# One state in four of a selective scan gets its input from TensorE instead of GpSimd, and several buffers are shared

## The chip, the cores and the metric

The kernel runs on one core of a Trainium2 chip. The metric is the device time of one execution in microseconds (us); less is better. PE is TensorE (PEld its weight loads), DVE is VectorE, ACT is ScalarE, POOL is GpSimd, SP is SyncE, which here does nothing but issue transfers. Each engine works through its own queue in order. PE writes its results to PSUM, which has eight banks of 128 partitions x 512 fp32 values.

## The reference

The input is x of 16 batches x 512 positions x 256 channels. Two layers follow each other: a selective state space model run in both directions, and a mixture of experts with soft slots; each is added to its input and normalised. Cut to what matters here:

```python
xr = x @ in_proj_w.T                     # 512 channels xf, 512 channels res
xf = silu(causal_conv(xf)); xb = silu(causal_conv(xf, other weights))
for u, reverse in ((xf, False), (xb, True)):
    dt, B, C = ...                       # dt: softplus, per channel; B, C: 16 states per position
    dA  = dt[l, d] * A[d, n]             # decay
    dBu = dt[l, d] * u[l, d] * B[l, n]   # what is added at each position
    h   = scan over l of exp(dA) * h + dBu     (with a damping factor)
    y  += sum over n of h[l, d, n] * C[l, n] + u * D
x1 = layernorm(x + (y * silu(res)) @ out_proj_w.T)
# then: 16 experts x 64 slots, softmax dispatch, gated expert layers, softmax combine, layernorm
```

So for each batch, direction, channel and state there is one scan over the 512 positions.

## The kernel before

Channels lie on the 128 partitions, the 512 positions along the free axis. The 512 channels are four chunks `c` of 128. For each batch `b` the function `scan_part` is called four times: chunks 0 and 1 forward (`r` = 0) and backward (`r` = 1), then chunks 2 and 3 forward and backward. A part goes through the 16 states two at a time (`n` = 0, 2, ..., 14). One *step* is one chunk and two states, so there are 64 steps in a batch and 1024 in all. A step does this:

- SP loads the two states' rows of B and C, broadcast over the partitions, into `bs` (three buffers) and `cs` (two buffers); one load serves two steps (L349).
- POOL forms `db` = `du` * `bs` for both states in one product of 128x1024 (L353); `du` = dt * u was made once per chunk and direction (L301).
- For each of the two states ACT writes the decay exp(A * dt) into a PSUM bank `h` (L358) and the damping factor `th` into SBUF (L360), DVE scans in place in that bank, `h` = scan(`h`, `db`) (L362 forward, L364 backward), and DVE forms `hg` = (`th` + 1) * `h` in SBUF (L367). The banks for `h` are a ring of three; `hg` has four buffers.
- POOL multiplies both states' `hg` by `cs` (L368).
- PE adds the product up over the states by eight transposes into the accumulator bank `acc` (L317); `add_up(2)` puts that two steps behind. Once in a chunk and direction PE adds u * D with a diagonal matrix `diagD` (L330): full fp32 products of 128x128.

The eight PSUM banks are: three for `h`, two for `acc`, three (`bank`) for everything else.

All the other work is cut into pieces by generators: `prep` (projections, convolution `taps`, B and C through `project_unit`, and dt, `rr`, `du` through `prep_pair` for the next part), `front` (`finish` of the batch before: output projection, normalisation, `dispatch` into slots) and `back` (`experts` of two batches, `combine` of each). `beside_scan` takes pieces of these after each step. Expert and combine work runs from batch 3 on; before that there is only `prep` and `front`. What is left of it after the last scan is the tail. A scheduler of the language places the instructions on each engine's queue from this program order, buffers and its own estimate of times; `late` fixes the place of the marked ones.

Buffers that the change touches: the x tile of a batch is loaded once and kept (two buffers) from `prep_forward` to `finish`; expert weights `W` have three buffers of 4 KB a partition; the slot embeddings `se` and the expert outputs `ceo` in `combine` share one of 8 KB; `et` and `sl` in `dispatch` have one each, `yt` in `finish` two.

Of the kernel before, what the change touches and what calls it, by code (L numbers as in the profile page):

```python
# [28 lines left out]
KW = 4  # L29
NE = 16  # L30
SL = 64
NSL = NE * SL
# [23 lines left out]
def seq_layers(tc, ident, neghalf, a, out):  # L56
# [17 lines left out]


    nc = tc.nc
    nb = a["x"].shape[0]
    with ExitStack() as ctx:
# [3 lines left out]
        s_dram = drams.tile([nb, NM, P, NSL], F32, name="s_dram")  # L82
        e_dram = drams.tile([NE, nb * SL, DM], F32, name="e_dram")
        const = ctx.enter_context(tc.tile_pool(name="m_const", bufs=1))
        p1 = ctx.enter_context(tc.tile_pool(name="m_p1", bufs=1))
# [19 lines left out]
        def load_x(b):  # L105
            xt = p2.tile([P, NL, DM], F32, tag="x", name=f"x_{b}")
            nc.sync.dma_start(xt, a["x"][b].rearrange("(c p) d -> p c d", p=P))
            return xt

        xs = {0: load_x(0)}  # L110


        outT = const.tile([P, ND, DM], F32, name="outT")
        zeros = const.tile([P, L], BF16, name="zeros")
        nc.vector.memset(zeros, 0.0)

        unit = const.tile([XW, 1], F32, name="unit")
# [69 lines left out]
        def prep_forward(b, lo, hi, out):  # L187

            xt = xs[b]
            if lo == 0:  # L190
                out["xT"] = p1.tile([P, NM, L], F32, tag="xT", name=f"xT_{b}")
                for k in range(NM):
                    yield 1
                    pt = bank(f"ptx_{b}_{k}")
                    for lc in range(NL):
                        nc.tensor.transpose(
                            pt[:, lc * P : (lc + 1) * P], xt[:, lc, k * P : (k + 1) * P], ident
                        )
                    yield HOLD
                    late(nc.scalar.copy(out["xT"][:, k, :], pt))  # L200
                out["u"] = p1.tile([P, ND, L], F32, tag="xf", name=f"xf_{b}")
            xT, xf = out["xT"], out["u"]
            for c in range(lo, hi):
                yield 1
                pp = project(xT, c, f"pin_{b}_{c}")
                yield HOLD
                taps(xf[:, c, :], pp, side[0], c, xf[:, c, :])
            if hi == ND:
                yield 0
                late(nc.scalar.activation(xf, xf, AF.Silu))  # L210
                yield from project_unit(b, 0, out)
# [25 lines left out]
        def project_unit(b, r, out):  # L237

            w = side[r]
            q = f"{b}_{r}"  # L240
            yield 1
            px = bank(f"px_{q}")
            for c in range(ND):
                nc.tensor.matmul(  # L244
                    px[:XW, :], w["xT"][:, c, :], out["u"][:, c, :], start=(c == 0), stop=(c == ND - 1)
                )
            yield HOLD
            xd = p1.tile([XW, L], F32, tag=f"xd_{r}", name=f"xd_{q}")
            bc = dram.tile([2, NS, L], F32, tag="bc", name=f"bc_{q}")
            if r == 0:  # L250
                late(nc.scalar.activation(xd, px[:XW, :], AF.Identity, bias=unit))
            else:

                late(nc.scalar.activation(xd[: XB + NS, :], px[: XB + NS, :], AF.Identity, bias=unit[: XB + NS]))
                nc.scalar.copy(xd[XC:XW, :], px[XC:XW, ::-1])
            nc.sync.dma_start(bc[0], xd[XB : XB + NS, :])
            nc.sync.dma_start(bc[1], xd[XC:XW, :])
            out.update(xd=xd, bc=bc)

        def prep_pair(b, r, p, v, gate=None):  # L260
# [27 lines left out]
            for c, q, pz in pzs:  # L288
# [12 lines left out]
                nc.gpsimd.tensor_tensor(du, dt, v["u"][:, c, :], ALU.mult)  # L301
                v[c] = (dt, rr, du)

# [34 lines left out]
        def scan_part(b, r, p, v, accs, done, then):  # L338

            prep.drain()  # L340
            prep.gens += [[1, g] for g in then]
            w = side[r]
            for n in range(0, NS, 2):
                q = f"{b}_{r}_{p}_{n}"

                bs = p3.tile([P, 2, L], F32, tag="bs", name=f"bs_{q}")
                cs = p3.tile([P, 2, L], F32, tag="cs", name=f"cs_{q}", bufs=2)
                for t, rows in ((bs, v["bc"][0, n : n + 2, :]), (cs, v["bc"][1, n : n + 2, :])):
                    nc.sync.dma_start(t, rows.unsqueeze(0).to_broadcast([P, 2, L]))  # L349
                for c in (2 * p, 2 * p + 1):  # L350
                    dt, rr, du = v[c]
                    db = p3.tile([P, 2, L], F32, tag="db", name=f"db_{q}_{c}")
                    nc.gpsimd.tensor_tensor(db, du.unsqueeze(1).to_broadcast([P, 2, L]), bs, ALU.mult)  # L353
                    hg = p3.tile([P, 2, L], F32, tag="hg", name=f"hg_{q}_{c}", bufs=4)
                    for j in range(2):
                        s = slice(n + j, n + j + 1)
                        h = ps_h.tile([P, L], F32, tag="h", name=f"h_{q}_{c}_{j}")
                        nc.scalar.activation(h, dt, AF.Exp, scale=w["A"][:, c, s])  # L358
                        th = p3.tile([P, L], F32, tag="th", name=f"th_{q}_{c}_{j}")
                        nc.scalar.activation(th, rr, AF.Tanh, bias=LN_1E12 / 2, scale=w["Ah"][:, c, s])  # L360
                        if r == 0:
                            nc.vector.tensor_tensor_scan(h, h, db[:, j, :], 0.0, ALU.mult, ALU.add)  # L362
                        else:
                            nc.vector.tensor_tensor_scan(  # L364
                                h[:, ::-1], h[:, ::-1], db[:, j, ::-1], 0.0, ALU.mult, ALU.add
                            )
# [3 lines left out]
                        (r == n == 0, n == 0, r == 1 and n == NS - 2, c, hg, accs, w, v["u"], f"acc_{q}_{c}", done)  # L370
                    )
                    evict()
                    beside_scan()
# [74 lines left out]
        def moe_setup():  # L448
# [4 lines left out]
            for t in (sg, sb):  # L453
                nc.vector.tensor_scalar(t, t, scale, None, ALU.mult)
            se = p1.tile([P, NSC, DM], F32, tag="ceo", name="se")
            nc.sync.dma_start(se, a["slot_embeds"].rearrange("e (s) d -> (e s) d").rearrange("(c p) d -> p c d", p=P))
            yield 0
            mv, rs = row_stats(nc, p1, se, neghalf, "se")
            sh = shifts(mv, rs, "se")
            yield 0  # L460
            scaled(se, se, sh, rs)
            for k in range(NM):
                for h in range(NSC // 4):
                    yield 1
                    pt = bank(f"pse_{k}_{h}")
                    for j in range(4):
                        nc.tensor.transpose(
                            pt[:, j * P : (j + 1) * P], se[:, h * 4 + j, k * P : (k + 1) * P], ident
                        )
                    yield HOLD  # L470
# [3 lines left out]
            for key in ("bg", "bu"):  # L474
                rows = p1.tile([NE * NF, P], F32, tag="et", name=f"{key}_rows")
                nc.sync.dma_start(rows, a[key].rearrange("e (c p) -> (e c) p", p=P))
# [23 lines left out]
        def finish(b, y):  # L500

            xt = xs.pop(b)
            for h in range(NL // 2):
                yts = []
                for lc in (2 * h, 2 * h + 1):
# [6 lines left out]
                    yield HOLD  # L512
                    yt = p2.tile([P, L], F32, tag="yt", name=f"yt_{b}_{lc}")
                    late(nc.scalar.copy(yt, pt))
# [49 lines left out]
        def dispatch(b, xn, x2T):  # L564

            for sc in range(NSC):
# [9 lines left out]
                late(nc.vector.reduce_max(nm, pl, AX.X, negate=True))  # L576
                et = p1.tile([P, L], F32, tag="et", name=f"et_{i}")
                sm = p3.tile([P, 1], F32, tag="sm", name=f"sm_{i}")
# [15 lines left out]
                if sc % 2 == 1:  # L594
# [12 lines left out]
                    yield HOLD  # L607
                    sl = p1.tile([P, NM, 256], F32, tag="sl", name=f"sl_{i}")
                    for k in range(NM):
# [137 lines left out]
        def combine(b):  # L747


            eo = p1.tile([P, NSC, DM + 1], F32, tag="ceo", name=f"ceo_{b}")  # L750
            nc.gpsimd.memset(eo[:, :, DM : DM + 1], 1.0)  # L751
            own = e_dram[:, b * SL : (b + 1) * SL, :]
            for j in range(2):
                nc.sync.dma_start(
                    eo[j * SL : (j + 1) * SL, :, :DM],
                    own.rearrange("(c j) s o -> j s c o", j=2)[j],
                )
            x1 = p1.tile([P, NL, DM], F32, tag="cx1", name=f"cx1_{b}")
# [7 lines left out]
            x2 = load_x2(0)  # L766
            yield 0
            prev = []

# [8 lines left out]
            for lc in range(NL):  # L778
# [40 lines left out]
                for sc in range(NSC):  # L819
                    nc.tensor.matmul(  # L820
                        po[:, : DM + 1],
                        cts[sc // 4][:, sc % 4 * P : (sc % 4 + 1) * P],
                        eo[:, sc, :],
                        start=(sc == 0),
                        stop=(sc == NSC - 1),
                    )
# [15 lines left out]
        for b in range(nb):  # L842
# [21 lines left out]
            if b + 1 < nb:  # L864
                xs[b + 1] = load_x(b + 1)
                then.append(prep_forward(b + 1, 0, 2, nxt))
# [64 lines left out]
```

## Time and profile before

| What | Value |
|---|---|
| Time, median of 3 runs | 5519.68 us (5513.75 to 5530.24) |
| Profiled execution: time | 5517.41 us |
| Profiled execution: span | 5515.6 us |
| PE busy, share of the span | 4004.2 us, 73% |
| DVE busy | 4522.2 us, 82% |
| ACT busy | 4097.3 us, 74% |
| POOL busy | 4998.6 us, 91% |
| Granted PE clock, mean | 0.861 |
| Data moved by transfers | 897.76 MB, mean 163 GB/s |

Busy is the time in which an engine was executing at least one instruction. The profile's rows have the line of the kernel, the engine, the operation, output and inputs by name, shapes and count, then the busy time and the mean length of one in ns, then how long the engine had idled just before them and what ended that idling. "A <- B" in a list of waits means that A's instruction was waiting and B's ended it; behind it stand the sum in us, how many times, and the longest. Matmuls overlap in their pipeline, so their mean length is longer than busy time over count. The chain of waits follows the work that ended last back to the start. The 40 slices give busy tenths per slice of 138 us.

### The profile page before, as it was taken

How to read it: one execution, taken by the hardware profiler on the slowest of the kernel's cores; microseconds unless marked ns; L12 is line 12 of the kernel's file. 1: busy time of each engine (PE TensorE's matmuls, PEld its weight loads, DVE VectorE, ACT ScalarE, POOL GpSimd, SP SyncE). 2: the span in 40 equal slices, each digit the busy share in tenths (PEclk: the TensorE clock that was granted, in tenths of full speed). 3: DMA queues.
4: the chain of work that ended last, by engine and by line, in shares of the span. 5: the costliest groups of instructions: out<-in, count | busy, mean ns of one | idle time of the engine just before them, and what ended most of it. 6: DMA issues, size and time to landing. Idle time of an engine off the chain costs nothing.

```text
span 5515.6 us, 67752 instructions
## 1 busy us (share of the span) xinstructions
PE 4004.2 (73%) x21330; PEld 3097.9 (56%) x21330; DVE 4522.2 (82%) x6210; ACT 4097.3 (74%) x6662; POOL 4998.6 (91%) x2525
## 2 busy tenths in 40 slices
PE   4556656777777777777777777777777777877777
PEld 3434444666556655666555655566556556566565
DVE  7787878888888889889888888888898898888512
ACT  6667677778778887878878787788778788777522
POOL 6999999999999999999999999999999999989500
PEclk7667777888988989888998899989899889999998
DMA  4333333565445654465545654456544665467253
GB/s 132 112 108 126 121 117 124 167 199 188 157 138 195 203 193 140 144 207 193 172 139 173 203 191 151 147 190 203 186 144 146 203 195 172 137 212 240 83 161 96
DMA packets 493852, 897.76 MB, mean 163 GB/s; under 512 B 44307, under 2 KB 291731, under 8 KB 493493
## 3 DMA queue, kind: packets, MB, share of 16 engines
q1 hardware_dynamic: 454836, 851.48, 47.6%
q10 hardware_dynamic: 38656, 41.95, 2.2%
q8 instruction: 169, 2.77, 0.2%
q14 instruction: 191, 1.56, 0.1%
HBM read 832.47 MB, written 60.82 MB: 162 GB/s over the span
## 4 chain that ended last, share of the span: by engine, by line
DVE 34%; ACT 24%; PE 18%; issue 11%; POOL 10%; DMA 3%; SPq 0%; DVEq 0%; ACTq 0%; POOLq 0%
DVE h L364 9%; DVE h L362 9%; DVE hg L367 8%; ACT h L358 5%; ACT th L360 5%; POOL hg L368 4%; POOL db L353 4%; PE acc L317 3%; PE px L244 2%; DVE rr L299 2%; PE cl L785 2%; PE pg L709 2%; ACT L358 2%; PE cpo L820 1%; ACT ht L731 1%
## 5 line engine op out<-in xcount | busy, mean ns | idle before, releaser
L353 POOL TENSOR_TENSOR db<-du,bs 128x1024 f32<-128x1024 f32 x1024 | 2431.3, 2374 | 113.8 <-DVE h L362 48.6
L368 POOL TENSOR_TENSOR hg<-hg,cs 128x1024 f32<-128x1024 f32 x1024 | 2427.6, 2371 | 25.4 <-DVE hg L367 17.6
L367 DVE SCALAR_TENSOR_TENSOR hg<-th,h 128x512 f32<-128x512 f32 x2048 | 1352.3, 680 | 251.1 <-ACT th L360 139.9
L317 PE MATMUL acc<-ident,hg 128*128 128x128 f32 x8192 | 1214.9, 301 | 391.4 <-POOL hg L368 316.0
L317 PEld LDWEIGHTS acc<-ident,hg 128*128 128x128 f32 x8192 | 1069.2, 157 | 634.1 <-POOL hg L368 410.9
L364 DVE TENSOR_TENSOR_SCAN h<-h,db 128x512 f32<-128x512 f32 x1024 | 1227.2, 1221 | 191.0 <-ACT h L358 155.2
L362 DVE TENSOR_TENSOR_SCAN h<-h,db 128x512 f32<-128x512 f32 x1024 | 1222.8, 1221 | 180.6 <-ACT h L358 131.7
L358 ACT ACTIVATE h<-dt,A_f 128x512 f32<-128x512 f32 x1024 | 699.9, 683 | 319.2 <-DVE hg L367 316.5
L358 ACT ACTIVATE h<-dt,A_b 128x512 f32<-128x512 f32 x1024 | 700.0, 684 | 292.6 <-DVE hg L367 290.9
L360 ACT ACTIVATE th<-rr,Ah_b 128x512 f32<-128x512 f32 x1024 | 728.0, 711 | 0.3
L360 ACT ACTIVATE th<-rr,Ah_f 128x512 f32<-128x512 f32 x1024 | 726.9, 710 | 0.2
L694 PE MATMUL peo<-Wd,ht 128*128 128x256 f32 x1024 | 314.8, 461 | 190.4 <-DVE ht L678 129.4
L694 PEld LDWEIGHTS peo<-Wd,ht 128*128 128x128 f32 x1024 | 223.2, 227 | 263.1 <-DVE ht L678 143.3
L709 PE MATMUL pg<-st,Wg 128*128 128x128 f32 x2048 | 277.7, 297 | 85.5 <-ACT xb L219 40.6
L785 PE MATMUL cl<-seT,cx 128*128 128x512 f32 x512 | 279.4, 689 | 75.3 <-DVE rr L299 36.7
L709 PEld LDWEIGHTS pg<-st,Wg 128*128 128x128 f32 x2048 | 265.7, 211 | 97.2 <-ACT xb L219 42.1
L666 PE MATMUL pu<-st,Wu 128*128 128x128 f32 x2048 | 270.2, 288 | 33.3 <-ACT ht L731 11.8
L666 PEld LDWEIGHTS pu<-st,Wu 128*128 128x128 f32 x2048 | 257.5, 203 | 57.0 <-ACT ht L731 16.8
L571 PE MATMUL pl<-x2T,seT 128*128 128x512 f32 x512 | 261.1, 634 | 22.9 <-DVE xf L168 12.5
L600 PE MATMUL pq<-dis,xn 128*128 128x256 f32 x1024 | 253.8, 405 | 15.7 <-ACT dis L590 13.0
L820 PE MATMUL cpo<-ceo,ct 128*128 128x257 f32 x1024 | 249.3, 398 | 21.9 <-ACT ct L814 17.0
L751 POOL MEMSET ceo<- 128x8 f32 x16 | 2.0, 124 | 260.4 <-PE cpo L820 259.4
(146 smaller groups left out, 5356.6 us busy)
## 6 DMA issues: line engine op xcount, KB each, us to landing
bs<-bc SPq DMA_DIRECT2D x512, 512.0 KB, 4.6
cs<-bc SPq DMA_DIRECT2D x512, 512.0 KB, 3.7
Wg<-in_Wg_dram SPq DMA_DIRECT2D x128, 512.0 KB, 5.4
Wu<-in_Wu_dram SPq DMA_DIRECT2D x128, 512.0 KB, 5.7
Wd<-in_Wd_dram SPq DMA_DIRECT2D x128, 512.0 KB, 5.6
bd<-in_bd_dram SPq DMA_DIRECT2D x128, 128.0 KB, 4.7
s_dram<-sl ACTq DMA_DIRECT2D x64, 256.0 KB, 2.9
st<-s_dram SPq DMA_DIRECT2D x128, 128.0 KB, 4.3
```

The costliest lines, as they stand in the source:

```text
L317: ins = nc.tensor.matmul(accs[c][:, s], hc[:, j, s], ident, is_transpose=True, start=False, stop=(last and j == 1 and lc == NL - 1),)
L353: nc.gpsimd.tensor_tensor(db, du.unsqueeze(1).to_broadcast([P, 2, L]), bs, ALU.mult)
L358: nc.scalar.activation(h, dt, AF.Exp, scale=w["A"][:, c, s])
L360: nc.scalar.activation(th, rr, AF.Tanh, bias=LN_1E12 / 2, scale=w["Ah"][:, c, s])
L362: nc.vector.tensor_tensor_scan(h, h, db[:, j, :], 0.0, ALU.mult, ALU.add)
L364: nc.vector.tensor_tensor_scan(h[:, ::-1], h[:, ::-1], db[:, j, ::-1], 0.0, ALU.mult, ALU.add)
L367: nc.vector.scalar_tensor_tensor(hg[:, j, :], th, 1.0, h, ALU.add, ALU.mult)
L368: nc.gpsimd.tensor_tensor(hg, hg, cs, ALU.mult)
L666: nc.tensor.matmul(pu[:, fc * P : (fc + 1) * P], got["Wu", e][:, k, fc * P : (fc + 1) * P], st[:, k, :, j * SL : (j + 1) * SL], start=(k = ...
L694: nc.tensor.matmul(po[:, :DM], ht[:, fc, :], got["Wd", e][:, fc, :], start=(fc == 0), stop=(fc == NF - 1))
L709: nc.tensor.matmul(pg[:, fc * P : (fc + 1) * P], got["Wg", e][:, k, fc * P : (fc + 1) * P], st[:, k, :, j * SL : (j + 1) * SL], start=(k = ...
L785: nc.tensor.matmul(cl, x2[:, k, :], seT[:, k, h * 512 : (h + 1) * 512], start=(k == 0), stop=(k == NM - 1),)
```

## The change

For one state in four (n = 3, 7, 11, 15) PE makes dt*u*B instead of POOL. `du` is transposed once per chunk and direction into `duT` (positions on partitions), and multiplied by diagonal matrices of B, one of 128x128 for each quarter of the positions. The result lands in an `h` bank; ACT writes the decay to an SBUF tile `dec`, and DVE scans with the bank as the addend, in place. The diagonal matrices come from a DRAM array that is zero but for its diagonals: it is filled with zeros at the start, `project_unit` writes the four states' rows of B onto the diagonals by one transfer of 2048 words, and `scan_part` loads the matrix of one state into `dg` once in four steps. In every second pair of states POOL's `db` product and the load of `bs` cover one state only.

To make room, x has one buffer and is loaded twice per batch; the slot embeddings and `combine`'s expert outputs are cut into pieces that use the buffers of `W`; `yt`, `et`, `sl` and the bias rows share two buffers `fr`; `combine`'s column of ones is set by DVE.

```diff
+        diag_dram = drams.tile([2, NS // 4, NL, DIAG_SIZE], F32, name="diag_dram")   # DIAG = 3, DIAG_SIZE = P * (P + 1)
...
         def load_x(b):
-            xt = p2.tile([P, NL, DM], F32, tag="x", name=f"x_{b}")
+            xt = p1.tile([P, NL, DM], F32, tag="x", name=f"x_{b}")
...
+        blank = p2.tile([P, 4 * DM], F32, tag="W", name="blank", bufs=3)
+        nc.vector.memset(blank, 0.0)
+        for part in diag_dram.rearrange("r i l (p s) -> (r i) p l s", p=P):
+            nc.scalar.dma_start(part, blank[:, : NL * (P + 1)].rearrange("p (l s) -> p l s", l=NL))
...
         def prep_forward(b, lo, hi, out):
-            xt = xs[b]
             if lo == 0:
+                xt = load_x(b)
...
         def project_unit(b, r, out):
...
             nc.sync.dma_start(bc[1], xd[XC:XW, :])
+            nc.scalar.dma_start(
+                diag_dram[r].rearrange("i l (p s) -> i l p s", p=P)[:, :, :, 0],
+                xd[XB + DIAG : XB + NS : 4, :].rearrange("i (l p) -> i l p", p=P),
+            )
...
         def prep_pair(b, r, p, v, gate=None):
...
-                v[c] = (dt, rr, du)
+                v[c] = [dt, rr, du]
+            yield 0
+            yield 0
+            yield 2
+            pts = []
+            for c, q, pz in pzs:
+                pt = bank(f"pdu_{q}")
+                for lc in range(NL):
+                    nc.tensor.transpose(pt[:, lc * P : (lc + 1) * P], v[c][2][:, lc * P : (lc + 1) * P], ident)
+                pts.append(pt)
+            yield HOLD
+            for (c, q, pz), pt in zip(pzs, pts):
+                duT = p2.tile([P, L], F32, tag="duT", name=f"duT_{q}", bufs=4)
+                late(nc.scalar.copy(duT, pt))
+                v[c].append(duT)
...
         def scan_part(b, r, p, v, accs, done, then):
+            made = {}
+            def by_diagonal(n, c):
+                made[n, c] = h = ps_h.tile([P, L], F32, tag="h", name=f"h_{b}_{r}_{n}_{c}")
+                for lc in range(NL):
+                    s = slice(lc * P, (lc + 1) * P)
+                    ins = nc.tensor.matmul(h[:, s], v[c][3][:, s], dg[:, s], start=True, stop=True)
+                    if lc == 0:
+                        late(ins)
+            chunks = (2 * p, 2 * p + 1)
             for n in range(0, NS, 2):
+                diag = n % 4 + 1 == DIAG
+                k = 2 - diag
-                for t, rows in ((bs, v["bc"][0, n : n + 2, :]), (cs, v["bc"][1, n : n + 2, :])):
-                    nc.sync.dma_start(t, rows.unsqueeze(0).to_broadcast([P, 2, L]))
-                for c in (2 * p, 2 * p + 1):
-                    dt, rr, du = v[c]
+                nc.sync.dma_start(bs[:, :k, :], v["bc"][0, n : n + k, :].unsqueeze(0).to_broadcast([P, k, L]))
+                nc.sync.dma_start(cs, v["bc"][1, n : n + 2, :].unsqueeze(0).to_broadcast([P, 2, L]))
+                if not diag:
+                    dg = p2.tile([P, L], F32, tag="dg", name=f"dg_{q}")
+                    nc.sync.dma_start(
+                        dg.rearrange("p (l s) -> p l s", l=NL),
+                        diag_dram[r, n // 4, :, : P * P].rearrange("l (p s) -> p l s", p=P),
+                    )
+                for c in chunks:
+                    dt, rr, du = v[c][:3]
-                    nc.gpsimd.tensor_tensor(db, du.unsqueeze(1).to_broadcast([P, 2, L]), bs, ALU.mult)
+                    nc.gpsimd.tensor_tensor(
+                        db[:, :k, :], du.unsqueeze(1).to_broadcast([P, k, L]), bs[:, :k, :], ALU.mult
+                    )
                     for j in range(2):
-                        h = ps_h.tile([P, L], F32, tag="h", name=f"h_{q}_{c}_{j}")
-                        nc.scalar.activation(h, dt, AF.Exp, scale=w["A"][:, c, s])
+                        if j < k:
+                            dec = h = ps_h.tile([P, L], F32, tag="h", name=f"h_{q}_{c}_{j}")
+                            add = db[:, j, :]
+                        else:
+                            add = h = made.pop((n + j, c))
+                            dec = p2.tile([P, L], F32, tag="dec", name=f"dec_{q}_{c}")
+                        nc.scalar.activation(dec, dt, AF.Exp, scale=w["A"][:, c, s])
...
-                            nc.vector.tensor_tensor_scan(h, h, db[:, j, :], 0.0, ALU.mult, ALU.add)
+                            nc.vector.tensor_tensor_scan(h, dec, add, 0.0, ALU.mult, ALU.add)
...
+                    if c == chunks[0] and diag:
+                        by_diagonal(n + 1, chunks[1])
+                    elif c == chunks[1] and not diag:
+                        by_diagonal(n + 3, chunks[0])
                     evict()
...
         def finish(b, y):
-            xt = xs.pop(b)
+            xt = load_x(b)
...
-            eo = p1.tile([P, NSC, DM + 1], F32, tag="ceo", name=f"ceo_{b}")
-            nc.gpsimd.memset(eo[:, :, DM : DM + 1], 1.0)
+            for c0 in range(0, NSC, 3):
+                m = min(3, NSC - c0)
+                t = p2.tile([P, 4 * DM], F32, tag="W", name=f"ceo_{b}_{c0}", bufs=3)
...
+            for t in eos:
+                late(nc.vector.memset(t[:, :, DM : DM + 1], 1.0))
```

## The prediction

> **What bounds the kernel now.** I read the page's totals and slices first, then busy times by stage, then the waits of each stage, then the chain. Totals and slices:
>
> ```profile
> PE 4004.2 (73%) x21330; PEld 3097.9 (56%) x21330; DVE 4522.2 (82%) x6210; ACT 4097.3 (74%) x6662; POOL 4998.6 (91%) x2525
> ...
> POOL 6999999999999999999999999999999999989500
> PEclk7667777888988989888998899989899889999998
> ```
>
> By these POOL is the bound: it is full from the second slice until the scan ends near 5190 us. The next two views contradict it for most of the span. Busy times of a stage early in the run (400 to 1000 us) and one after the expert work has joined (1000 to 4280 us); in brackets the instructions:
>
> ```profile
> 400.00:1000.00 600.00, 371.74 (x1670) 272.63 (x1669) 496.60 (x600) 430.85 (x675) 587.10 (x291) 0.73 0.36 121
> 1000.00:4280.00 3280.00, 2481.39 (x13654) 1938.88 (x13653) 2878.28 (x3949) 2617.71 (x4258) 3191.18 (x1602) 0.89 0.54 174
> ```
>
> The columns are PE, PEld, DVE, ACT, POOL, granted clock, DMA. A step (one channel chunk, two states) has 8 transposes at L317; the view of that line counts 976 in the early window and 5232 in the late one, so 122 and 654 steps: 4.92 and 5.02 us a step. A late step holds 4.88 us of POOL, 4.40 of DVE, 4.00 of ACT, 3.79 of PE. What PE waits for, early, then late:
>
> ```profile
> PE acc L317 <- POOL hg L368: 140.2, 61, 5.9
> PE acc L317 <- POOL rr L298: 20.3, 8, 3.5
> PE pd L585 <- ACT et L581: 16.8, 6, 5.0
> ...
> PE pd L585 <- ACT et L581: 99.3, 35, 7.3
> PE ctp L809 <- ACT cm L802: 97.4, 35, 9.1
> PE peo L694 <- DVE ht L678: 93.7, 32, 5.2
> PE acc L317 <- POOL hg L368: 39.1, 32, 2.2
> ```
>
> Early, 160 of PE's 228 us of waiting are for POOL. Late, 70 of 799 are (39.1 and 30.4); the rest is PE, in order, standing before side work whose operand ACT or DVE has not finished. The chain agrees. Early, then late:
>
> ```profile
> by line: POOL db L353 13.1%; issue 12.1%; POOL hg L368 11.8%; DVE h L364 10.9%; DVE h L362 9.7%; DVE hg L367 7.4%; PE acc L317 4.4%; ACT th L360 3.8%; PE pq L600 3.8%; ACT h L358 3.6%; DVE rr L299 1.7%; PE pz L268 1.6%; ACT L358 1.3%; PE px
> ...
> by line: issue 11.2%; DVE h L364 9.3%; DVE hg L367 9.2%; DVE h L362 8.8%; ACT h L358 5.8%; ACT th L360 5.4%; POOL hg L368 3.1%; PE acc L317 3.0%; POOL db L353 2.6%; PE px L244 2.4%; DVE rr L299 2.2%; PE pg L709 2.0%; ACT L358 1.9%; PE cl L7
> ```
>
> POOL's two products hold 25% of the early chain and 6% of the late one. So POOL sets the pace for about three batches of 16 (192 steps); for the other 832 steps it is just busy enough, and the pace comes from the ring ACT `h`, DVE scan, DVE `hg`, ACT `h` over three PSUM banks, with PE's in-order queue beside it:
>
> ```profile
> ACT h L358 <- DVE hg L367: 355.7, 284, 3.6
> ```
>
> **The change, part by part.** Rows used:
>
> ```profile
> L353 POOL TENSOR_TENSOR db<-du,bs 128x1024 f32<-128x1024 f32 x1024 | 2431.3, 2374 | 113.8 <-DVE h L362 48.6 <-issue 45.7 <-DVE h L364 10.7
> L301 POOL TENSOR_TENSOR du<-dt,xb 128x512 f32<-128x512 f32 x64 | 80.3, 1278 | 0.0
> L330 PE MATMUL acc<-diagD_f,xf 128*128 128x128 f32 x512 | 76.7, 299 | 0.0
> L330 PE MATMUL acc<-diagD_b,xb 128*128 128x128 f32 x512 | 71.9, 286 | 0.0
> L585 PE MATMUL pd<-ident,et 128*128 128x128 f32 x512 | 96.5, 320 | 163.3 <-ACT et L581 149.0 <-DVE xf L168 14.3
> ```
>
> *POOL.* 512 of the 1024 `db` products shrink from 128x1024 to 128x512. The nearest half-size product is `du`: 2374 - 1278 = 1096 ns, times 512, is 561 us off POOL, 0.55 a step: 4.88 becomes 4.33.
>
> *PE.* 512 banks of four full fp32 products. L330 is the same shape and shows 1024 instructions where the code has 512 products, so two each: (76.7 + 71.9) / 128 = 1.16 us a bank, 594 us in all. `duT` adds 512 transposes, at 96.5 / 512 us 97 us. Together 691 us, 0.67 a step: 3.79 becomes 4.46. PE goes from the least to the most loaded engine of a late step. Of these 0.67 us nothing is on the path if they all fall into PE's waits (1.22 us a late step, 0.11 of it for POOL); all of it is if each wait keeps its length, because its operand starts from an earlier PE result that is now later too. Bounds 0 and 0.67 x 832 = 557 us. I take a third, 185: the waits are some 3 us long and come every two to three steps, so one of them can take up most of what was added since the last, and what remains delays the next side operand.
>
> The clock bears on this: 0.73 is granted where PE is busy 62%, 0.89 at 76%, and a transpose of L317 costs 0.183 us of PE in the first window (178.83 / 976), 0.139 in the second (724.62 / 5232). The Trainium skill ("TensorE: Matmul & The Clock Gate", Part 1) says that the array's clock is halved after idle windows and released by sustained work. By that rule a fuller PE comes to full clock, its late work shrinks by a ninth or 0.4 us a step, and the 185 would be near 70. By the rows the late stage is near full clock already, and I count nothing.
>
> *The banks.* A made bank is taken from the ring of three when PE fills it, one place ahead of an `h` that DVE reads sooner, and returned after it. I took both kernels' built instruction orders and summed, for each ACT `h`, DVE's work between the `hg` that frees its bank and the scan that needs it, at busy time over count (scan 1.20, `hg` 0.66 us). That cover falls short of a lone `h` (0.68 us) by 1 us in all before and 51 after; of an `h` behind one `th` (0.68 + 0.71) by 32 and 124; behind two such pairs (2.8) by 386 and 758. DVE's recorded waits for ACT `h`, 287 us, lie between the last two. So the added wait is between 50 and 372 us; I take the middle row, 92, as ACT mostly issues `h` and `th` in pairs. The made bank itself has 5.9 us of cover in the mean and is rarely late.
>
> *ACT.* 128 `duT` copies at 579 ns (L590, same shape), 74 us; 512 `dec` written to SBUF, at the 26 ns between `th` and `h` 13 us; 32 issues of the diagonal's write. A 512-element issue of 4 bytes takes 0.5 us on SP (`cb_f`), one of 256 pieces 0.37, so some 1.5 us for 2048: 48 us. Together 135 us; behind each issue stand Softplus and the next `h`. A third on the path, as for PE: 45; bounds 0 and 135.
>
> *Transfers.* `dg` takes the bytes that `bs` loses. It is queued on SP among loads that wait for POOL, about four steps (20 us) ahead of use against 4 to 5 us to land (`cx`, 512-byte pieces, 3.7): nothing; without that cover 256 x 4 us. The diagonal's write scatters 2048 words; 512 such words landed in 3.9 us (`cb_f`), so at most 16 us, inside the several steps before the first `dg`: nothing, except 0 to 10 us in the first batch. The skill ("DMA: Bandwidth & Descriptors", Specifications) puts full rate at 512 bytes and above, with read-modify-write below; by that rule the write is slow, and it would cost only if it outlasted those steps. Filling the blanks, the second `x` load (16 x 512 KB, needed three pieces later), weights and combine sharing W (at most 8 us at each of 7 hand-overs), `fr`, and 48 small memsets moved to DVE: 15 us with the head.
>
> *Gains.* Early, POOL's 0.55 us a step come off until DVE (4.07) and the rings bind; I take 0.3 of it, 192 steps: -60. Late, waiting for POOL per step is 0.11 on PE, 0.17 on ACT (`m_sh`, `c_sh`: 57.8 and 54.6 us) and little on DVE; these overlap, and a less full POOL queue removes about 0.12: -100; bounds 0 and -0.31 x 832 = -258.
>
> Sum against the profiled execution, 5517.4 us (span 5515.6), 2.3 us under the median of 5519.7: -60 - 100 + 185 + 92 + 45 + 15 = +177, so 5694, in the median's terms about 5695.
>
> **The rivals.** *POOL is the bound throughout* (faster). The slices speak for it; the late chain and the late waits against it. POOL leaves 0.55 us a step, DVE at 4.40 binds; half way from its present 88% to the 97% POOL has now, 92.5%, is 4.76 us: -0.26 x 832 - 60 = -276, 5240. It decides if, with POOL relieved, DVE's cover above is refilled by ACT running ahead. *Costs and relief nearly cancel on the good side*: PE's waits swallow all its new work and ACT's 45 vanish: 5695 - 185 - 45 = 5465. *PE becomes the pace*: every wait keeps its length, +557 instead of +185, 6065; for it speaks 4.46 busy plus 1.22 waiting against 5.02, against it the slack in those waits. *The change does not relieve POOL*, if the half product cost like the full one: `du` excludes it.
>
> **How the numbers follow.** 0.3% is 17 us, about what runs 16 us apart can tell. Forecast case (5560 to 5850) 0.52, PE's pace 0.10, POOL's bound 0.20, near cancellation 0.18, of which 0.06 fall within 0.3%. So faster 0.32, same 0.06, slower 0.62. The range reaches up to 5900 with part of PE's case out, and down to 5320 with about half of POOL's case out.
>
> **What would show it.** Right: POOL's `db` group near 1870 us and its late busy share under 90%; the made banks near 600 us of PE; DVE waiting more than 287 us for ACT `h`; PE's waits shorter but its share near 88%. The step on banks is wrong if DVE's share rises past 90%; that on PE if the early stage gains and the late stage keeps 5.02 us a step or less; the whole forecast if the late step falls to 4.8.

## The result, and the profile after

The changed kernel takes 5561.7 us (median of 4 runs, 5559.1 to 5564.0) against 5519.2 for the kernel before (4 runs on the same chip, 5513.8 to 5530.2): a ratio of 1.0074, 95% interval 1.0057 to 1.0092. The change costs 42 us. The prediction said 5695, so the sign is right, the time lies just inside the 5560 to 5850 of its forecast case, and the cost is 133 us too large: 176 us against 42.

Totals and slices of the changed kernel, as shown of before:

```profile
PE 4374.8 (79%) x25938; PEld 3539.5 (64%) x25938; DVE 4514.5 (81%) x6259; ACT 4170.1 (75%) x6783; POOL 4462.7 (80%) x2513
...
POOL 5999899888879788897888888798888979878400
PEclk8778888899999999998998999999899989999999
```

POOL has lost 536 us and is seldom at 9 tenths after the seventh slice. PE has gained 371 us, while the new work on it holds 666 us (made banks 588.3, transposes of `du` 77.9, predicted 691), so the old work takes some 295 us less. The granted clock rose with it, from 0.861 to 0.910: the clock row is higher than before in 18 slices of 40 and lower in none. The busy times of the two stages, same columns as before (PE, PEld, DVE, ACT, POOL, granted clock, DMA share, GB/s):

```profile
400.00:1000.00 600.00, 419.73 (x2354) 337.77 (x2353) 520.67 (x637) 471.43 (x740) 550.68 (x303) 0.84 0.42 131
1000.00:4280.00 3280.00, 2684.87 (x16322) 2186.48 (x16321) 2829.54 (x3918) 2614.60 (x4255) 2804.66 (x1569) 0.93 0.56 174
```

The view of L342, the transposes that were L317, counts 1008 and 5168 instructions in these windows: 126 and 646 steps, 4.76 and 5.08 us a step (before 4.92 and 5.02). The early stage gained, the late one lost. A late step now holds 2684.87 / 646 = 4.16 us of PE, not the predicted 4.46.

The groups that the prediction spoke of (busy time and mean ns of one, then the idle time ahead of them and what ended it):

```profile
L398 POOL TENSOR_TENSOR db<-du,bs 128x1024 f32<-128x1024 f32 (+1 forms) x1024 | 1867.8, 1825 | 565.2 <-DVE h L414 252.6
...
L342 PE MATMUL acc<-ident,hg 128*128 128x128 f32 x8192 | 1137.7, 286 | 94.0 <-POOL hg L420 61.3
...
L375 PE MATMUL h<-dg,duT 128*128 128x128 f32 x4096 | 588.3, 290 | 163.0 <-DVE hg L419 126.8
...
L414 DVE TENSOR_TENSOR_SCAN h<-dec,h 128x512 f32<-128x512 f32 x256 | 311.4, 1216 | 113.1 <-PE h L375 112.9
L416 DVE TENSOR_TENSOR_SCAN h<-dec,h 128x512 f32<-128x512 f32 x256 | 310.6, 1215 | 90.1 <-PE h L375 89.6
```

POOL's `db` (predicted near 1870) and the made banks on PE (594) are as sized. PE's idle time ahead of the transposes of L342, 391 us before, is 94. New are the last two rows: the scans whose addend is a made bank stand 202 us waiting for PE. The waits of DVE over the whole run (us in all, times, longest) put that beside the rest:

```profile
DVE csm L836 <- PE cpo L883: 120.3, 34, 8.2
DVE h L416 <- ACT h L410: 116.3, 81, 4.1
DVE h L414 <- PE h L375: 112.9, 47, 8.2
DVE h L416 <- PE h L375: 89.6, 39, 3.9
DVE h L414 <- ACT h L410: 85.8, 58, 3.7
```

Before, the rows for ACT's `h` were:

```profile
DVE h L364 <- ACT h L358: 155.2, 110, 9.8
...
DVE h L362 <- ACT h L358: 131.7, 87, 6.0
```

These waits, which the prediction expected to grow from 287 us, fell to 202. DVE's waits for made banks, which did not exist before, came to another 202 us, in 86 waits.

**Where they are.** I split each run at the starts of POOL's `hg` products, the 64th of which ends a batch (us counted from the trace's zero, 11 us ahead of the first instruction):

| kernel | first `hg` | batches 0 to 2 | batches 3 to 15 | from the last `hg` on | time of the profiled execution |
|---|---|---|---|---|---|
| before | 65.6 | 945.1 | 4181.2 | 335.0 | 5517.4 |
| changed | 80.1 | 888.1 | 4264.8 | 338.3 | 5562.3 |

So: head +14.5 (predicted +15), three early batches -57 (predicted -60), the late ones +84 (predicted +222), tail +3. Early and head came out near their numbers; what has to be explained is the late stage. It lost in every second batch: from batch 4 to 14 the even ones take 330 to 331 us, the odd ones 321, where before all took 319 to 321; the last takes 354 instead of 337. Within a batch the waits for made banks are not spread out: step 6 has 77.6 of the 202 us and step 54 has 60.7, one wait in each of the 16 batches. The timeline of the changed kernel at step 6 of batch 1, the longest of these waits (start, length, engine and line; idle time before it and what ended that; rows of other work left out):

```profile
372.31 1.28 ACT L232 ACT_TABLE_LOAD   x1
...
373.61 1.91 ACT L232 ACTIVATE xb<-xb 128x2048 f32<-128x2048 f32 x1
...
375.57 6.48 PE L251 MATMUL px<-xb,xpT_b 128*80 128x512 f32 x8 [10.35 <-ACT xb L232]
...
382.08 0.68 ACT L261 ACTIVATE xd<-px,unit 48x512 f32<-48x512 f32 x1 [4.73 <-PE px L251]
...
383.19 1.06 PE L375 MATMUL h<-dg,duT 128*128 128x128 f32 x8
...
384.29 1.23 DVE L414 TENSOR_TENSOR_SCAN h<-dec,h 128x512 f32<-128x512 f32 x1 [8.16 <-PE h L375]
```

PE comes to `px`, the projection to B, C and dt, while ACT still has to load a table and run Silu over all of `xb`. PE stands for 10.35 us, then `px` takes 6.48 us, then come transposes, and only then the made bank, at which PE does not idle any more. DVE stands for 8.16 us. Before the change no scan took an operand from PE, so PE could stand there without holding up a scan directly. In the even batches from 4 to 14 PE stands 9.62 us before this `px` and the bank is 6.6 to 7.1 us late; in the odd ones from 3 to 13 it stands 0.75 to 1.56 us, and the bank, behind `px` alone, is 2.2 us late. Step 54 stands behind the same projection, that of `xf` for the next batch: in batch 7 PE waits 4.60 us for Silu, `px` takes 5.88 us, and the scan stands 3.87 us.

### The profile page after: what moved, and what is told of

The parts are those of the page before. It is cut to its first block, busy times and chain, and to the rows that moved or that the text cites. A ratio compares the mean times of both kernels' runs of the same rounds, so it can differ in the third digit from the quotient of the medians.

```text
span 5560.4 us, 78299 instructions
## 1 busy us (share of the span) xinstructions
PE 4374.8 (79%) x25938; PEld 3539.5 (64%) x25938; DVE 4514.5 (81%) x6259; ACT 4170.1 (75%) x6783; POOL 4462.7 (80%) x2513
## 5 line engine op out<-in xcount | busy, mean ns | idle before, releaser
L398 POOL TENSOR_TENSOR db<-du,bs 128x1024 f32<-128x1024 f32 (+1 forms) x1024 | 1867.8, 1825 | 565.2 <-DVE h L414 252.6
L342 PE MATMUL acc<-ident,hg 128*128 128x128 f32 x8192 | 1137.7, 286 | 94.0 <-POOL hg L420 61.3
L342 PEld LDWEIGHTS acc<-ident,hg 128*128 128x128 f32 x8192 | 1010.7, 149 | 241.4 <-issue 81.2
L416 DVE TENSOR_TENSOR_SCAN h<-h,db 128x512 f32<-128x512 f32 x768 | 923.9, 1219 | 128.7 <-ACT h L410 116.3
L414 DVE TENSOR_TENSOR_SCAN h<-h,db 128x512 f32<-128x512 f32 x768 | 920.7, 1218 | 100.5 <-ACT h L410 85.8
L375 PE MATMUL h<-dg,duT 128*128 128x128 f32 x4096 | 588.3, 290 | 163.0 <-DVE hg L419 126.8
L410 ACT ACTIVATE h<-dt,A_f 128x512 f32<-128x512 f32 x768 | 523.6, 684 | 231.7 <-DVE hg L419 230.0
L375 PEld LDWEIGHTS h<-dg,duT 128*128 128x128 f32 x4096 | 532.3, 203 | 195.1 <-DVE hg L419 112.4
L410 ACT ACTIVATE h<-dt,A_b 128x512 f32<-128x512 f32 x768 | 525.2, 684 | 161.2 <-DVE hg L419 158.3
L414 DVE TENSOR_TENSOR_SCAN h<-dec,h 128x512 f32<-128x512 f32 x256 | 311.4, 1216 | 113.1 <-PE h L375 112.9
L416 DVE TENSOR_TENSOR_SCAN h<-dec,h 128x512 f32<-128x512 f32 x256 | 310.6, 1215 | 90.1 <-PE h L375 89.6
L754 PE MATMUL peo<-Wd,ht 128*128 128x256 f32 x1024 | 284.3, 426 | 102.8 <-ACT yt L574 49.7
```

What stands on the lines that cost most here:

```text
L342: ins = nc.tensor.matmul(accs[c][:, s], hc[:, j, s], ident, is_transpose=True, start=False, stop=(last and j == 1 and lc == NL - 1),)
L375: ins = nc.tensor.matmul(h[:, s], v[c][3][:, s], dg[:, s], start=True, stop=True)
L398: nc.gpsimd.tensor_tensor(db[:, :k, :], du.unsqueeze(1).to_broadcast([P, k, L]), bs[:, :k, :], ALU.mult)
L410: nc.scalar.activation(dec, dt, AF.Exp, scale=w["A"][:, c, s])
L414: nc.vector.tensor_tensor_scan(h, dec, add, 0.0, ALU.mult, ALU.add)
L416: nc.vector.tensor_tensor_scan(h[:, ::-1], dec[:, ::-1], add[:, ::-1], 0.0, ALU.mult, ALU.add)
```

## The experiments

The first four runs ask which part of the change costs; theory 1 is the prediction's reading with its terms, theory 2 the rival that POOL's work counts in every batch. The next ones ask how the banks cost: by PE's in-order queue, where they stand behind side work (Q), or by the ring of three `h` banks (R). Experiments 1 to 9 are one execution each; the four of the kernel before lie 16 us apart, so a difference below that is not told from none.

**1. The relief alone.** The kernel before, with POOL's `db` cut to one state in every second pair; the second state scans the first one's product, so the sums differ.

```diff
-    nc.gpsimd.tensor_tensor(db, du.unsqueeze(1).to_broadcast([P, 2, L]), bs, ALU.mult)
+    k = 2 - (n % 4 == 2)
+    nc.gpsimd.tensor_tensor(db[:, :k, :], du.unsqueeze(1).to_broadcast([P, k, L]), bs[:, :k, :], ALU.mult)
```

> The kernel before, but in every second pair of states POOL forms db for one state only (128x512) and both scans read that half; so one state in four gets another state's input. Nothing else changes: no made banks, no new PE or ACT work. It shows POOL's relief alone. Theory 1 (the prediction's reading, POOL sets the pace only in the first three batches; the costs of the change were sized too high): late relief 0.12 us a step, early 0.3, so about 5360 us, batches from 4 on near 313 us. Theory 2 (POOL sets the pace in most late steps too, those without convolution work; relief and costs are both large and cancel): late relief 0.3 to 0.5 us a step, so 5100 to 5230 us, batches from 4 on between 289 and 302 us.

Measured 5369.2, before 5515.8 beside it: -147, theory 1's number and far from theory 2's. Batches 0 to 2 take 869.1 (-76), the late ones 4112.7 (-68), the rest -4. So the relief is worth a little less than the predicted 160 (the early batches more than the 60 taken, with 19 us of costs there to set against it; the late ones less than the 100), and the late batches do not run at POOL's pace: POOL is busy 4459 us here and 4999 before, and some 440 us less of it in thirteen batches give them 68.

**2. The costs alone.** The changed kernel with POOL's product and the load of `bs` in full.

> The kernel after, but POOL forms db (and SP loads bs) for both states in full, as before; the fourth state's half is not used. It shows the costs without the relief. Theory 1: costs of about 180 us in the late stage and 15 at the head, so about 5700 us. Theory 2: costs of 320 us or more in the late stage, so 5820 us or more. If the costs lie where POOL waits anyway, less than 5640.

Measured 5665.6, 150 us over before: under theory 1's number, and further under theory 2's. The relief and the costs, each alone, add to +3, while the change is +42; so they do not simply add, but each is about 150, not the 160 and 337 of the prediction's sum.

**3. A cheaper bank.** The changed kernel, with most of a bank's fp32 products replaced by one bf16 product of zeros over the whole bank; the made state's addend is left out but for 128 positions.

```diff
-    for lc in range(NL):
-        s = slice(lc * P, (lc + 1) * P)
-        ins = nc.tensor.matmul(h[:, s], v[c][3][:, s], dg[:, s], start=True, stop=True)
-        ...
+    late(nc.tensor.matmul(h, zeros[:, :P], zeros, start=True, stop=False))
+    nc.tensor.matmul(h[:, :P], v[c][3][:, :P], dg[:, :P], start=False, stop=True)
```

> The kernel after, but a made bank is filled by one bf16 product of zeros over 512 columns and one fp32 product of 128 columns instead of four fp32 products; the fourth state's input is left zero for three quarters of the positions. Order of the banks, waits on dg and duT, transposes and POOL's work are as after; only about 0.6 us of PE work per made bank is gone (300 us in all). If PE's new work is what costs: 5410 to 5460 us. If the order of the banks in the ring or ACT's queue is what costs: within 30 us of 5562.

Measured 5537.7, 24 us under the changed kernel, where 100 to 150 were expected if PE's work were the cost. Its groups on PE:

```profile
L374 PE MATMUL h<-dg,duT 128*128 128x128 f32 x1024 | 213.1, 293 | 2.3
...
L373 PE MATMUL h<-zeros 128*128 128x512 bf16 x469 | 193.6, 413 | 223.5 <-DVE hg L416 215.6 <-DMA Wg<-in_Wg_dram 5.3 <-DMA dg<-diag_dram 2.5
```

406.7 us instead of 588.3: 182 us of work taken off PE, fewer than the 300 expected, give 24, an eighth. (43 of the 512 bf16 products are missing in the trace; and PE's busy time as a whole fell by 141 us only, as its clock fell to 0.887. By that it is a sixth.) DVE still waits 198 us for the banks (107.6 and 90.3). So the length of a bank's products is a small part of it; the next two runs ask for its place.

**4. The buffers alone.** The kernel before with x, weights and outputs sharing buffers, all made banks, diagonals and transposes of `du` left out.

> The kernel before with the shared buffers alone: one x buffer loaded twice, weights, slot embeddings and combine outputs in the W buffers, fr, the ones set by DVE; no made banks, POOL in full. Even batches from 4 on are 10 us longer in the kernel after and odd ones are not, and even batches hold the two combines. If the shared buffers make that: even late batches near 331 us, odd near 320.5, the last batch near 355, in all about 5600 us with the head. If the made banks make it: every batch within 2 us of before, so 5519 to 5540.

Measured 5528.7, +13, inside the spread. The late batches take 4186.3 (+5) and the first `hg` comes 2.7 us later. Sharing is nearly free.

**5. `px` later in PE's order.** Two empty places (a place is one call of the side work, once a step) before `px`:

```diff
+            yield 0
+            yield 0
             yield 1
             px = bank(f"px_{q}")
```

> The changed kernel, with the projection px (four fp32 products that need the whole Silu of xb or xf) put into PE's order two scan steps later, by two empty places before it. Theory Q (queue): the loss is made banks that stand in PE's in-order queue behind px, while px waits for ACT's Silu; in the changed kernel DVE waits 78.9 us for a made bank at step 6 of the 16 batches, one wait of 4.9 us in each, all behind px. Then those waits fall under 20 us and the time is 60 to 90 us under the changed kernel's 5562: 5470 to 5500. Theory R (ring): the loss is the third bank of the ring, which the made state holds while ACT's next h waits for it. Then it stays within 15 us of 5562.

Measured 5459.5: 102 us under the changed kernel, more than the 60 to 90 expected, and 58 under the one before (5517.2 beside it). Rows of DVE's waits in this kernel:

```profile
DVE h L418 <- PE h L377: 61.6, 27, 5.1
...
DVE h L416 <- PE h L377: 44.2, 33, 5.1
```

106 us instead of 202; at step 6 the waits fell from 77.6 us to 5.2, and PE stands at most 1.1 us before `px` of `xb`. The late batches take 4170.5, 94 less; the even ones from 4 to 14 are at 317 to 320 us, the odd ones still at 319 to 322. The place in a queue, with no work removed, is worth more than twice what the whole change cost. R predicted no gain here.

**6. The ring.** The changed kernel, with the made state scanned first of its pair, so that its bank returns sooner (`for j in (1, 0) if diag else (0, 1):`).

> The changed kernel, with the made state scanned first of its pair and not second, so that its bank comes back to the ring one scan and one hg product (1.9 us) sooner. Worked out on the order of instructions, DVE's cover for ACT's h then falls short by 8, 38 and 404 us instead of 51, 124 and 758 (before: 1, 32, 386). Theory R (ring): 40 to 90 us faster than 5562, 5470 to 5520. Theory Q (queue): each made bank is needed 1.9 us sooner, so the waits for it grow from 202 us by 1.9 us at each of some 60 to 130 late banks, 100 to 250 us: slower, 5640 to 5780.

Measured 5587.2, 25 us slower than the changed kernel. The gain that R forecast did not come. It is not Q's number either: the waits for made banks did not grow (rows of DVE's waits):

```profile
DVE h L414 <- PE h L375: 111.1, 51, 7.4
...
DVE h L416 <- PE h L375: 77.8, 53, 4.4
```

189 us, of which 76.0 at step 6 and 40.1 at step 54. My 1.9 us for each late bank was wrong; the long wait at step 6 hardly depends on which scan is first. DVE's waits for ACT's `h` did fall, from 202 to 156 us, so the ring is a part of them; but its waits for `th` and `acc` ahead of `hg` grew from 70 to 108. All its waits add up to 979 us here and 981 in the changed kernel, its busy time is 15 us longer. Why, and where the 25 us come from, stays open.

**7. The same places in the kernel before.**

> The kernel before, with the same two empty places before px. There no scan waits for PE, so by both theories it moves nothing that DVE or POOL wait for: within 15 us of 5516. If it comes out over 40 us faster, px's place costs every kernel here and is no cost of the change.

Measured 5547.3, 30 us slower than before; I had expected nothing. DVE's waits for ACT are 40 us longer (531 against 491). A later `px` makes `xd`, dt and B later; that this is what costs was not shown. So the gain in experiment 5 is no general one: it needs the changed kernel, and may be net of such a cost.

**8. Made banks in three batches only.** The changed kernel, x loaded first, and for `b >= 3` no diagonals, no transposes of `du`, no products into banks, POOL's `db` whole (`diag = b < 3 and n % 4 + 1 == DIAG`, and the same condition at each of the other places).

> The changed kernel with made banks in batches 0 to 2 alone (diagonals written, transposes of du and the bank's products are left out after; POOL's db is whole there), and the first x loaded ahead of the weights. The first three batches took 56.9 us less in the changed kernel, and its head 14.5 us more. If the later loss comes from the made banks, by Q or by R, the later batches go back to 320.5 us each: 5516 - 57 + 0 to 10 for the blanks, 5455 to 5475. If it comes from what the change moves besides (shared buffers, combine's loads and memsets), the even batches keep 10 us more: 5500 to 5530.

Measured 5494.2, between the two expectations. The late batches are back at 4188.5 (before 4181.2), the early ones at 892.0. So the late loss belongs to the made banks with what feeds them, and not to the buffers. What I had wrong is the head: the first `hg` still comes at 81.1, with x in front. The timeline of this kernel has the first two weights of `in_proj` issued by SP at

```profile
23.31 0.98 SPq L187 DMA_DIRECT2D w_pin<-in_in_projT_dram  x2
```

against 12.39 in the kernel before (19.20 in the changed kernel, which loads x behind the small weights). ACT's queue sends 2.1 MB of blanks at the start, and SP's issues beside them come with gaps.

**9. The head.** The changed kernel with x first and the eight blank writes on SP behind the first projections' loads.

> The changed kernel with x loaded first and the eight blank writes (2.1 MB) moved from the start of ACT's queue to SP, behind the loads of the first projections. In the kernel that kept made banks for three batches x stood first too, and POOL's first hg still came at 81.1 us (before 65.6, changed 80.1), with SP's issues of the weights spread out to 34 us instead of 24. If the blanks cost the head by taking the transfers' time from the weights, the first hg comes at 65 to 69 us and the time falls by 10 to 16 us to 5546 to 5552. If the head is late for the diagonal's write, the first dg or the transposes of du, it stays at 77 us or more and the time at 5556 to 5566.

The first `hg` comes at 71.0, 9 us sooner, and SP issues the first two weights at 12.66; x in front alone had not moved the head (experiment 8), so the blanks were most of it. It is later than the 65 to 69 expected, and the 10 to 16 us did not come: the time is 5562.3, as the late batches take 4273.0, 8 us more than in the changed kernel. Why they do was not shown; a single execution does not separate a loss of 8 us from none.

**10 to 12. A version that beats both.** `px` two places later with the head of 9; one place instead of two; and two places with the diagonal's writes issued by SP (`nc.sync.dma_start` in `project_unit`).

> The kernel with px two places later, and the blanks and x moved as in the run on the head. With px later it measured 5459.5; if the two add up it gives 5443 to 5452, 1.2 to 1.4% under the kernel before. If the made banks' waits come back because the head is shifted against the side work, 5480 or more.

> The same with one empty place before px instead of two. Silu and its table load take 3.2 us of ACT, a step 4.7 to 5.0 us. Theory Q: one place lets Silu end before PE comes to px, if ACT begins it at once; then the time is within 12 us of the kernel with two places (5435 to 5460), and the end of the batch, where the side work now runs on (tail 353 us against 338), may give some 10 us back. If ACT begins Silu a step late, behind th and h, half of the 78.9 us of waits at step 6 come back: 5480 to 5500.

> The kernel with two places, blanks and x moved, and the 32 writes of the diagonal issued by SP and not by ACT. ACT's issues take 0.65 us each, 21 us in all. The prediction put a third of ACT's new work on the path: 7 us faster than with ACT's issues. If all of it is, 21 us; if ACT's queue has room there, within 4 us. SP holds the two bc writes that wait for the same xd, so no wait is added there.

| kernel | time, median of 4 (lowest, highest) | ratio to before (5519.8), 95% interval | batches 3 to 15 | DVE waits for made banks |
|---|---|---|---|---|
| two places | 5441.5 (5439.6, 5447.2) | 0.9859, 0.9845 to 0.9874 | 4175.6 | 111 |
| one place | 5481.7 (5481.4, 5483.6) | 0.9931, 0.9915 to 0.9948 | 4207.7 | 80 |
| two places, SP writes | 5428.3 (5425.9, 5432.5) | 0.9835, 0.9820 to 0.9849 | 4157.5 | 85 |

Two places came out 2 us below the expected span. SP's writes give 13 us more, between the third and the whole of ACT's 21 us. One place met the number for half a cure, 5480 to 5500, but not by the waits that I named: they are fewer than with two places. The batches tell: from batch 4 on those with an odd number take 315 us (two places: 319 to 321), those with an even one 330 (two places: 317 to 323), but for the last. The even ones hold the second half of an expert group and the combines. The timeline of the kernel with one place, in batch 8 near step 6:

```profile
2554.98 3.60 PE L255 MATMUL px<-xb,xpT_b 128*80 128x512 f32 x5
...
2558.42 1.95 PE L730 MATMUL pu<-st,Wu 128*128 128x128 f32 x16
...
2560.41 1.13 DVE L742 SCALAR_TENSOR_TENSOR ht<-pu,bu_cols,ht 128x128 f32<-128x128 f32 x4 [3.40 <-PE pu L730]
2561.08 1.06 PE L379 MATMUL h<-dg,duT 128*128 128x128 f32 x8
```

DVE stands 3.40 us for `pu`, a product of the experts that lies behind `px` too, and the scans stand behind that instruction in DVE's queue. The same delay of PE reaches DVE by another operand, and the row of waits for made banks does not show it. Over the run the row `ht` <- `pu` has 47.4 us here and 27.8 with two places. That this makes all of the 10 us by which an even batch is longer was not shown.

## Why the prediction was right or wrong

**Right.** POOL's late share under 90% (85.5%), the sizes of `db` (1867.8 us) and of the made banks (588.3), and the reading that POOL does not set the late pace: experiment 1 takes some 540 us of work off POOL and gains 68 in thirteen batches, against the 100 taken. The three early batches (-57 against -60) are partly luck: their relief is 76 us, not 60, and 19 us of costs, taken as nothing, stand against it. So is the 15: the head alone took 14.5, and the shared buffers, which that term held too, 13 in experiment 4.

**The step that failed in the sum: PE, banks and ACT in the late stage, 185 + 92 + 45 = 322.** Measured, as the changed kernel's late batches against those with the relief alone, 4264.8 - 4112.7, the whole change but for its relief costs 152 us there (125 in experiment 2, where POOL has its full product). That is 170 us too many in the sum; the late relief, taken 32 us too large, and some 5 us elsewhere stand against it, and what is left is the 133 us. By term:

- *PE's work, 185.* "A third" of 557 us is on the path, said the step. Experiment 3 gives an eighth (24 of 182); an eighth of 557 is 73. And the 557 were too many: a late step gained 0.36 us of PE, not 0.67, because the old work got shorter. The transposes of L342 take 692.96 / 5168 = 0.134 us each late and 155.89 / 1008 = 0.155 early, 0.139 and 0.183 before, at a clock of 0.93 and 0.84 instead of 0.89 and 0.73.
- *The banks, 92.* The ring was priced from DVE's cover for ACT's `h`. DVE's waits for ACT's `h` fell by 85 us instead, and experiment 6, which gives that cover back, takes another 46 us off them and is slower as a whole. No run shows the 92.
- *ACT, 45.* The 32 issues took 0.65 us each, not 1.5: 21 us, and moving them off ACT gave 13 (experiments 10 and 12).

How the 152 us divide among these, the transfers and the next was not measured.

**The step that failed in the mechanism: "The made bank itself has 5.9 us of cover in the mean and is rarely late."** It was put at nothing. It is late at 86 places, by 202 us, and two thirds of that is at two steps of each batch. The mean hid it: PE doesn't stand evenly. The trace of before held the row, in the view of PE's waits (in all, times, longest):

```profile
PE px L244 <- ACT xb L225: 95.5, 16, 10.5
```

16 times in 16 batches, 6 us in the mean and up to 10.5, more than a cover of 5.9. Read as "PE waits, so its new work can hide there", it went into the sum as a reason for a lower price; read as "whatever DVE needs from PE stands here too", it would have put a price of up to 95 us on `px` alone. The waits at step 6 came to 77.6, and moving `px` took 102 us off the whole. So a cost was there, as forecast, but another one than those priced: that the sign is right is in part luck, for the two errors stand against each other.

DVE's idle time sums up who it waits for, with DVE's own work the same in all (4514 to 4522 us). Added up over the view of DVE's waits, in us, beside the time of the same execution ("all" holds up to 15 us of others):

| kernel | for PE | for ACT | for DMA | for POOL | all | time |
|---|---|---|---|---|---|---|
| before | 278 | 491 | 63 | 75 | 917 | 5517.4 |
| relief alone | 284 | 401 | 63 | 15 | 774 | 5369.2 |
| changed | 509 | 337 | 108 | 14 | 981 | 5562.3 |
| two places before `px` | 377 | 345 | 114 | 23 | 870 | 5459.5 |
| two places, SP writes | 362 | 344 | 110 | 24 | 849 | 5432.5 |

The relief takes 60 us from POOL and 90 from ACT. The rest of the change puts 225 on PE and 45 on DMA (29 of it `ceo`, the combine's loads through `W`, and its column set by DVE) and takes another 64 from ACT; after that, moving `px` takes back 132 of PE's 225. Of the rivals, POOL as the bound throughout needed 216 us from the late batches, and experiment 1, with no cost beside it, gives 68; PE's pace needed all of PE's work on the path, and experiment 3 puts an eighth there. The near cancellation, 5465, had all of PE's new work in PE's waits, and experiment 3 shows that for seven eighths of what it took off; what it lacked, like the forecast, were the waits for made banks. Experiment 5, without most of them, is at 5459.5.

**The signs it named.** It said that the step on PE is wrong if the early stage gains and the late one keeps 5.02 us or less: the late step is 5.08, so it came near that. Two of its signs of being right failed: that DVE waits more than 287 us for ACT's `h` (202), and that PE's late share is near 88% (2684.87 of 3280, 82%).

**The rule it weighed.** The Trainium skill ("TensorE: Matmul & The Clock Gate", Part 1) says that idle windows halve the array's clock and sustained work releases it; by that the prediction would have taken some 0.4 us a late step back and 70 for the 185. The old work did come out 0.3 us a step shorter, so the rule was the better guide here than the row of 0.89 that I took for "near full". The trace agrees at `px` of `xb`, in the view of that line (lowest, median and highest ns of one product):

```profile
L251 PE MATMUL px<-xb,xpT_b x128: 592/593/1143, 88.8 to 4900.9; 128*80 128x512 f32 x128
```

In the ten batches where PE had stood 4.4 us or more, the first product takes 1139 to 1143 ns and those after it some 1060, and from the fifth to the eighth on they take 593; in the six where it had stood 1.6 us or less, the first takes 657 and the others 592. With `px` two places later the highest is 657.

**Open.** The best kernel is 59 us above the relief alone. DVE's waits name 47 more us at transfers there (`ceo` 34, `bd` 13), and 31 us of waits for made banks are left at step 54. In batch 7 the bank stands there behind the transposes of `et`, for which PE waits 5.84 us in the same way, and an expert product of 4.76 us. Neither was tried.

## What to carry to other kernels

When work moves to an engine that had slack, price the place and not the work alone: list that engine's long waits in the old trace, and ask what the new consumer's operand will stand behind. A mean cover says little where the queue stands in the same two spots of every batch. Before undoing such a change, move the side operation that stands in front: here two empty places in the order made a loss of 0.7% into a gain of 1.1%, and the diagonals' writes and the head brought it to 1.65%.

## What the runs showed of the hardware that was not expected

- With more PE work the granted clock rose (0.861 before, 0.887 in experiment 3, 0.910 after), and nearly half of the added work was made up by shorter old work: 666 us added, 371 more busy.
- A write of 2048 single words was issued in 0.65 us (1.21 us the first time), hardly more than the 0.50 us of the load of 512 words (`cb_f`).
- 2.1 MB of writes on ACT's queue at the start pushed SP's issue of the first weights from 12.4 to 19.2 us, and to 23.3 with x loaded first; with the writes moved behind, it was at 12.7.
